# Turning the last three feed-forward tiles with VectorE and small DMAs instead of TensorE, in a fused cross-attention and feed-forward kernel

## The chip, the cores and the metric

The kernel runs on one core of a Trainium2 chip. The metric is device time in microseconds (us): the median of several runs, lower is better. The engines of the core are TensorE (PE), VectorE (DVE), ScalarE (ACT), GpSimd (POOL) and SyncE (SP, which only issues DMAs here).

## What is computed

One transformer block over 1024 tokens (16 sequences of 64) of width 512, in float32: cross-attention with 32 heads of width 128, and a feed-forward layer with a routed low-rank part. The reference, cut to what matters:

```python
x = x + xattn(layernorm(x), ctx, mask, bias, Wq, Wk, Wv, Wo)
x = x + ffn(layernorm(x), ...)

def ffn(x, base_W, base_b, router_W, router_b, A, B, expert_map):
    base_out = einsum('btd,od->bto', x, base_W) + base_b
    logits = einsum('btd,nd->btn', x, router_W) + router_b      # 15 logits
    probs = softmax(logits)
    topk_p, topk_i = top_k(probs, 8)
    w = einsum('btk,btke->bte', topk_p, onehot(expert_map[topk_i]))
    h = einsum('btd,erd->bter', x, A)                           # 8 experts, rank 16
    lora = einsum('bter,eor->bto', h * w[..., None], B) * 2.0
    return base_out + lora
```

## The kernel before

Nearly all of the time goes to the attention projections. The change touches only the last stage, the feed-forward layer.

Tokens are split into eight tiles of 128 (`NT = 8`). For a matmul the normalised tile `xn` (128 tokens by 512) must stand with its width along the partitions, so it is turned: four TensorE transposes of 128x128 into one PSUM bank (`transposed`, line 104, called by `ffn_in`). `split` (lines 70 and 71) then makes two float32r tiles of it: `x2h`, a rounded copy written by ACT, and `x2l`, the rest, written by DVE. Every product is three matmuls (high x high, high x low, low x high).

One tile t goes through these steps:

- `ffn_norm(t)` (lines 700 to 720) and `ffn_apply(t)` (lines 721 to 726): layer norm of the attention's result `acc`. For tiles 5 to 7 the sums are made on ACT and the reciprocal root on POOL (lines 717 and 718).
- `turned(t)`: `ffn_bias` on POOL (line 729, `xb = acc + bias`), then `ffn_in`, the transposes and the split.
- `first(t)`: 12 matmuls of 256 columns (A), the low-rank and router products and the first 112 output columns (line 742).
- `ffn_route` on DVE and ACT (lines 753 to 757): logits, their maximum, exponentials. `ffn_weight` on DVE (lines 762 to 773): the eight best, the experts' weights, and `hw`, the weighted low-rank activations.
- 12 matmuls of 400 columns (B, the rest of the output), `ffn_turn` between them (line 779: one TensorE transpose of `hw`, split into `hh` on ACT and `hl` on DVE), and six matmuls with `hh` and `hl` (`ffn_lora`).
- `ffn_out` (lines 794 to 798): two DVE adds into `o1`, and a DMA to `out` issued by SP.

The stage is software-pipelined by hand. Inside `tc.manual_schedule` each engine runs its instructions in the order in which the program lists them. Round t of the last loop turns tile t+2, does `first` for tile t+1 and finishes tile t:

```python
for t in range(NT):
    turned(t + 2)
    first(t + 1)
    ...
    hh, hl = ffn_turn(hw)
    ffn_mm(po, *x2s[t], B, range(n, KC))
    if 5 <= t + 4 < NT:
        ffn_apply(t + 4)
    if 5 <= t + 5 < NT:
        ffn_norm(t + 5)
```

So in one round ACT runs, in this order: x2h of tile t+2, the exponentials of tile t+1, hh of tile t, then the norms of later tiles. DVE runs x2l, the logits, hl, the routing weights, and the two output adds. Pools give `x2h`, `x2l` and `xb` three buffers and `xn` four.

The same turn by DVE and DMAs is used in the attention stage for `xT` (`x_turn`, lines 330 and 333): one DVE transpose of 32x32 blocks, then 16 DMAs, all issued by POOL, move the blocks to their partitions. SP issues DMAs of a similar kind for the attention's probabilities (`turned_p`, line 505).

Of the kernel before, what the change touches and what calls it, by code (L numbers as in the profile page):

```python
# [9 lines left out]
F32 = mybir.dt.float32  # L10
# [9 lines left out]
P = 128  # L20
D = 512
KC = D // P
H = 32
NT = 8
# [23 lines left out]
def xattn_ffn_kernel(ctx: ExitStack, tc: tile.TileContext, x, ctxT, wq, wk, wv, wo, fside, mask,  # L48
                     base_wT, base_b, arT, router_b, lora_b, expert_map, out):
    nc = tc.nc  # L50
# [12 lines left out]
    def bank(k=None):  # L63
        return psp.tile([P, 512], F32, tag="ps", name="ps")
# [4 lines left out]
    def split(hi, lo, src, lo_eng=None):  # L69
        first = nc.scalar.copy(hi, src)  # L70
        return first, (lo_eng or nc.vector).tensor_tensor(lo, src, hi.bitcast(F32), ALU.subtract)  # L71
# [30 lines left out]
    def transposed(ps, xn):  # L102
        for kc in range(KC):
            nc.tensor.transpose(ps[:, kc * P:(kc + 1) * P], xn[:, kc * P:(kc + 1) * P], ident)  # L104
# [4 lines left out]
    with ExitStack() as actx:  # L109
# [240 lines left out]
        with tc.manual_schedule(engines={nc.tensor.engine}):  # L350
# [159 lines left out]
            def pv_mm(i, pt, v, home="o"):  # L510
                ps = [bank() for _ in range(2)]
                for t in range(NT):
                    for a in range(2):
                        r = slice(a * S, (a + 1) * S)
                        for d in range(0, P, S):
                            c = slice(i * P + d, i * P + d + S)
                            nc.tensor.matmul(ps[a][d:d + S, t * S:(t + 1) * S], lhsT=v[t // 2][r, t % 2, c],  # L517
                                             rhs=pt[r, :, t, :], start=True, stop=True)
                res = []
                for b in range(2):  # L520
                    hl = [blk(home, f"o{c}", F32R) for c in "hl"]
                    with tc.high_priority(offset=SOON):
                        evicted[:] = split(hl[0], hl[1], ps[b])
                    res.append(hl)
                return res

            def proj_o(t, cts, w):
                ps = bank()
                b, g = divmod(t, 4)
                c = slice(g * P, (g + 1) * P)  # L530
                for i, ct in enumerate(cts):
                    mm3(ps, [a[:, c] for a in ct[b]], w[i], i == 0, i == 1)
                with tc.high_priority(offset=SOON):
                    return nc.vector.tensor_tensor(acc[:, t, :], acc[:, t, :], ps, ALU.add)  # L534
# [59 lines left out]
            w, prev, added, pts, soft, ss, ns, t = None, None, None, [], [], [], 0, 0  # L594
# [12 lines left out]
            for p in range(NP):  # L607
# [3 lines left out]
                for c in steps:  # L611
                    if c == "P":
                        old, told = prev, t
                        prev, t = ([pv_mm(i, pts[i], v, "g" if p + 1 == NP else "o") for i in range(2)], w), 0
# [66 lines left out]
    fs2 = ctx.enter_context(tc.tile_pool(name="fs2", bufs=2, reuse_waits="tile"))  # L681
    psf = ctx.enter_context(tc.tile_pool(name="psf", bufs=2, space=PSUM, reuse_waits="tile"))
# [17 lines left out]
    def ffn_norm(t):  # L700
        xt = acc[:, t, :]
        xns[t] = xn = fs2.tile([P, D], F32, tag="xn", name="xn2", bufs=4)
        st = fs2.tile([P, 5], F32, tag="st", name="st", bufs=4)
        total, nm, sq, rs, nb = (st[:, i:i + 1] for i in range(5))
        if t < 5:
            with tc.high_priority(offset=SOON):
                bs = fs2.tile([P, 6], F32, tag="bs", name="bs")
                nc.vector.bn_stats(bs, xt)  # L708
                nc.vector.bn_aggr(st[:, 0:2], bs)
                nc.vector.tensor_scalar(rs, nm, EPS, None, ALU.add)  # L710
                nc.gpsimd.tensor_tensor(rs, rs, nhalf[:, 0:1], ALU.pow)  # L711
                nc.vector.scalar_tensor_tensor(nb, total, -1.0, rs, ALU.mult, ALU.mult)
        else:
            nc.scalar.activation(xn, xt, AF.Identity, accum_out=total)
            nc.scalar.activation(nm, total, AF.Identity, scale=-1.0 / D)
            nc.scalar.activation(xn, xt, AF.Square, bias=nm, accum_out=sq)
            nc.gpsimd.tensor_scalar(rs, sq, 1.0 / D, EPS, ALU.mult, ALU.add)
            nc.gpsimd.tensor_tensor(rs, rs, nhalf[:, 0:1], ALU.pow)
        stats[t] = nm, rs, nb

    def ffn_apply(t):
        nm, rs, nb = stats[t]
        if t >= 5:
            nc.scalar.activation(nb, nm, AF.Identity, scale=rs)
        nc.scalar.activation(xns[t], acc[:, t, :], AF.Identity, bias=nb, scale=rs)

    def ffn_bias(t):
        xb = fs2.tile([P, D], F32, tag="xb", name="xb", bufs=3)
        nc.gpsimd.tensor_tensor(xb, acc[:, t, :], bb, ALU.add)
        return xb  # L730

    def ffn_in(xn):
        ps = psf.tile([P, D], F32, tag="pt", name="pt")
        transposed(ps, xn)
        x2h = fs2.tile([P, D], F32R, tag="x2h", name="x2h", bufs=3)
        x2l = fs2.tile([P, D], F32R, tag="x2l", name="x2l", bufs=3)
        with tc.high_priority(offset=SOON):
            split(x2h, x2l, ps)
        return x2h, x2l

    def mm(o, a, b, start=False, stop=False):
        nc.tensor.matmul(o, lhsT=a, rhs=b, start=start, stop=stop, skip_group_check=True)  # L742

    def ffn_mm(o, x2h, x2l, w, kcs=range(KC)):
        for kc in kcs:
            c = slice(kc * P, (kc + 1) * P)
            mm(o, x2h[:, c], bh[:, kc, w], kc == 0)
            mm(o, x2h[:, c], bl[:, kc, w])
            mm(o, x2l[:, c], bh[:, kc, w], stop=kc == KC - 1)

    def ffn_route(pa):
        lg = fs2.tile([P, NR], F32, tag="lg", name="lg")
        nc.vector.tensor_tensor(lg, pa[:, E * R:NAR], rb, ALU.add)
        nm = fs2.tile([P, 1], F32, tag="nm", name="nm")
        nc.vector.tensor_reduce(nm, lg, AX.X, ALU.max, negate=True)
        sme = fs2.tile([P, 1], F32, tag="sme", name="sme2")
        nc.scalar.activation(lg, lg, AF.Exp, bias=nm, accum_out=sme)
        return pa, lg, sme
# [18 lines left out]
    def ffn_turn(hw):  # L777
        pt = psf.tile([P, D], F32, tag="pt", name="pt")
        nc.tensor.transpose(pt[:, 0:P], hw.rearrange("p e r -> p (e r)"), ident)
        hh = fs2.tile([P, P], F32R, tag="hh", name="hh")  # L780
        hl = fs2.tile([P, P], F32R, tag="hl", name="hl")
        with tc.high_priority(offset=SOON):
            split(hh, hl, pt[:, 0:P])
        return hh, hl

    def ffn_lora(o, hh, hl, w):
        mm(o, hh, lbh[:, w])
        mm(o, hh, lbl[:, w])
        mm(o, hl, lbh[:, w], stop=True)

    def ffn_out(t, xb, pa, po):
        o1 = fs2.tile([P, D], F32, tag="o1", name="o1", bufs=4)
        for c, src in ((slice(NA - NB, D), po), (slice(0, NA - NB), pa[:, NB:NA])):
            nc.vector.tensor_tensor(o1[:, c], xb[:, c], src, ALU.add)
            if t + 1 == NT:
                (nc.sync if c.start else nc.scalar).dma_start(out=out[t, :, c], in_=o1[:, c])
        if t + 1 < NT:
            nc.sync.dma_start(out=out[t], in_=o1)

    xns, xbs, x2s, pas, stats = ({} for _ in range(5))  # L800

    def out_norm(t):
        proj_o(t, *prev)
# [2 lines left out]
    def turned(t):  # L806
        if t < NT:
            xbs[t] = ffn_bias(t)
            x2s[t] = ffn_in(xns[t])

    def first(t):
        if t < NT:
            pas[t] = bank()
            ffn_mm(pas[t][:, A], *x2s[t], A)
# [17 lines left out]
    with tc.manual_schedule(engines=fixed | {nc.vector.engine}):  # L832
# [3 lines that stand above are left out]
            if t == 0:  # L836
                proj_o(7, *prev)
            if t + 1 < NT:
                r = ffn_route(pas[t + 1])
            n = 1 if t else 2  # L840
            po = bank()[:, 0:NF - NA]
            ffn_mm(po, *x2s[t], B, range(n))
# [6 lines that stand above are left out]
            if t + 1 < NT:  # L849
                hw = ffn_weight(*r)  # L850
            ffn_lora(po, hh, hl, B)
            ffn_lora(pas[t][:, A], hh, hl, A)
            ffn_out(t, xbs[t], pas[t], po)


# [40 lines left out]
```

## Time and profile before

| | |
|---|---|
| median of 3 runs | 762.75 us (762.65 to 764.97) |
| the profiled execution | 763.53 us |
| its span in the profile | 761.7 us |
| granted TensorE clock | 0.999 |
| DVE busy | 565.8 us, 74% of the span |
| ACT busy | 412.0 us, 54% |
| POOL busy | 194.8 us, 26% |
| the last loop, eight rounds | from 718.5 to 758.9 us |

The span is what the instruction trace covers; the execution is longer by the time around it. In the profile's lines PE is the matmul and PEld the weight load, which overlaps it; a letter q behind an engine (SPq, ACTq) is its sequencer, which issues DMAs and waits for semaphores. `L742` is line 742 of the kernel. In a timeline the columns are the start in us from the span's start, the length in us, the engine, the line, the operation, what it writes and reads, and a count; brackets give the idle time before it and what ended it. Matmuls are pipelined, so a row's length overlaps the next row.

### The profile page before, as it was taken

To read this page: it belongs to the slowest core of one execution; us is meant where nothing else is said; L and a number is where in the kernel's file an instruction comes from. 1 tells how busy PE (TensorE), PEld (TensorE's weight loads), DVE (VectorE), ACT (ScalarE), POOL (GpSimd) and SP (SyncE) were. 2 spreads that over 40 slices of the span, in tenths; PEclk is the share of its full clock that TensorE was granted. 3 is DMA by queue.
4 is the path that set the end of the run, shared out by engine and by line. 5 is a ranking of instruction groups with operands and counts; after the bars stand their busy time and mean duration, and the time that the engine had idled before them with its cause. 6 is when DMAs were issued, how large, how long until landed. Compare 5 with 4: busy or idle time off the path is not lost.

```text
span 761.7 us, 16780 instructions
## 1 busy us (share of the span) xinstructions
PE 752.5 (99%) x6154; PEld 624.9 (82%) x6154; DVE 565.8 (74%) x1076; ACT 412.0 (54%) x1157; POOL 194.8 (26%) x271
## 2 busy tenths in 40 slices
PE   8999999999999999999999999999999999999998
PEld 6888888888788888877888888888888888888898
DVE  7986567666655776869778777787778777878975
ACT  5654444444444445667645565456645765474361
POOL 0000008108820693223220222022211232010330
PEclk9999999999999999999999999999999999999999
DMA  6685647465735446466554465436544564462011
GB/s 255 229 285 186 205 157 229 147 218 179 224 130 187 156 126 225 142 222 217 189 158 149 138 199 167 142 120 201 174 141 134 180 185 140 125 199 84 1 57 56
DMA packets 84946, 126.79 MB, mean 166 GB/s; under 512 B 11776, under 2 KB 35072, under 8 KB 84864
## 3 DMA queue, kind: packets, MB, share of 16 engines
q1 hardware_dynamic: 80624, 123.56, 49.9%
q0 software_dynamic: 4096, 2.11, 1.2%
q8 instruction: 48, 0.79, 0.5%
q14 instruction: 34, 0.28, 0.1%
q10 hardware_dynamic: 144, 0.06, 0.0%
HBM read 83.74 MB, written 35.65 MB: 157 GB/s over the span
## 4 chain that ended last, share of the span: by engine, by line
PE 91%; DVE 3%; POOL 2%; DMA 2%; issue 1%; ACT 0%; SPq 0%; DVEq 0%; ACTq 0%; POOLq 0%
PE ps L259 73%; PE yz L259 5%; PE ps L742 5%; PE ps L517 4%; PE pss L470 4%; POOL xT L333 1%; DMA cT<-in_ctxT 1%; DMA so<-in_wo 0%; DMA xT<-xb 0%; DVE bs L708 0%; DVE gl L71 0%; PE pt L104 0%; DVE s L161 0%; DVE ol L71 0%; POOL st L711 0%
## 5 line engine op out<-in xcount | busy, mean ns | idle before, releaser
L481 ACT ACTIVATE p<-p,nm 128x64 f32<-128x64 f32 x256 | 85.9, 339 | 33.3 <-DVE nm L475 31.0
L534 DVE TENSOR_TENSOR acc<-acc,ps 128x512 f32<-128x512 f32 x128 | 86.8, 681 | 21.2 <-PE ps L259 20.4
L259 PE MATMUL ps<-wh,ol 128*128 128x512 f32 x256 | 99.9, 390 | 0.8 <-DVE ol L71 0.8
L259 PE MATMUL ps<-wh,oh 128*128 128x512 f32 x256 | 100.1, 391 | 0.0
L259 PE MATMUL ps<-wl,oh 128*128 128x512 f32 x256 | 99.7, 389 | 0.0
L70 ACT CAST gh<-s 128x512 fp32r<-128x512 f32 (+1 forms) x128 | 64.4, 514 | 56.0 <-PE ps L259 45.7
L333 POOL DMA_DIRECT2D xT<-xb x128 | 69.7, 552 | 84.9 <-DVE xb L330 80.7
L71 DVE TENSOR_TENSOR gl<-s,gh 128x512 fp32r<-128x512 f32 (+1 forms) x128 | 72.0, 566 | 23.2 <-ACT gh L70 23.1
L161 POOL TENSOR_TENSOR s<-rq 128x256 f32<-128x256 f32 x32 | 25.3, 790 | 238.9 <-DMA rq<-in_wq 190.1
L71 DVE TENSOR_TENSOR ol<-ps,oh 128x512 fp32r<-128x512 f32 x64 | 39.9, 683 | 31.5 <-ACT oh L70 31.3
L70 ACT CAST gh<-raw 128x512 fp32r<-128x512 f32 x48 | 29.8, 623 | 52.8 <-PE yz L259 36.1
L259 PEld LDWEIGHTS ps<-wh,ol 128*128 128x128 f32 x256 | 48.1, 188 | 11.4 <-DVE ol L71 1.6
L259 PEld LDWEIGHTS ps<-wl,oh 128*128 128x128 f32 x256 | 48.1, 188 | 10.0
L259 PEld LDWEIGHTS ps<-wh,oh 128*128 128x128 f32 x256 | 48.0, 188 | 10.0
L71 DVE TENSOR_TENSOR gl<-raw,gh 128x512 fp32r<-128x512 f32 x48 | 35.1, 731 | 27.9 <-ACT gh L70 20.7
L461 POOL TENSOR_TENSOR bm<-bm,maskb 128x512 f32<-128x512 f32 x32 | 42.4, 1348 | 36.6 <-DMA bm<-in_fside 36.6
L481 ACT ACTIVATION_READ_ACCUMULATOR p<-p,nm 128x1 f32 x256 | 48.6, 190 | 0.0
L565 DVE TENSOR_TENSOR q<-u,ps 128x512 f32<-128x512 f32 x48 | 32.8, 683 | 20.4 <-PE ps L259 16.0
L70 ACT CAST oh<-ps 128x512 fp32r<-128x512 f32 x64 | 33.2, 590 | 11.0 <-PE ps L517 11.0
L70 ACT CAST gh<-rq 128x256 fp32r<-128x256 f32 x48 | 19.5, 406 | 36.0 <-PE ps L259 32.1
L517 PEld LDWEIGHTS ps<-pt,v 64*64 64x64 f32 x2048 | 31.9, 135 | 5.7 <-issue 5.6
L554 ACT COPY u<-ps 128x512 f32<-128x512 f32 x48 | 27.9, 581 | 15.9 <-PE ps L259 8.8
(258 smaller groups left out, 1986.2 us busy)
## 6 DMA issues: line engine op xcount, KB each, us to landing
kd<-c SPq DMA_DIRECT2D x64, 256.0 KB, 2.6
vd<-c SPq DMA_DIRECT2D x64, 256.0 KB, 2.8
kT<-kd SPq DMA_DIRECT2D x64, 256.0 KB, 3.9
v<-vd SPq DMA_DIRECT2D x64, 256.0 KB, 3.7
raw<-in_wk SPq DMA_DIRECT2D x32, 256.0 KB, 4.0
raw<-in_wv SPq DMA_DIRECT2D x32, 256.0 KB, 4.3
rq<-in_wq SPq DMA_DIRECT2D x32, 256.0 KB, 4.1
bm<-in_fside SPq DMA_DIRECT2D x32, 256.0 KB, 4.5
```

Source lines behind the costliest of these rows:

```text
L70: first = nc.scalar.copy(hi, src)
L71: return first, (lo_eng or nc.vector).tensor_tensor(lo, src, hi.bitcast(F32), ALU.subtract)
L259: nc.tensor.matmul(o, lhsT=a, rhs=b, start=first and n == 0, stop=last and n == 2, skip_group_check=True)
L333: nc.gpsimd.dma_start(out=dst[32 * j:32 * j + 32, :, 32 * i:32 * i + 32], in_=xb[32 * i:32 * i + 32, j])
L461: nc.gpsimd.tensor_tensor(bm, bm, maskb, ALU.add)
L470: nc.tensor.matmul(ps[a * S:(a + 1) * S, t, :], lhsT=qT[n // 8][:, cq], rhs=kT[m // 8][:, ck], start=True, stop=True)
L481: nc.scalar.activation(p[:, t, :], p[:, t, :], AF.Exp, bias=nm[:, t:t + 1], accum_out=sme[:, t:t + 1])
L517: nc.tensor.matmul(ps[a][d:d + S, t * S:(t + 1) * S], lhsT=v[t // 2][r, t % 2, c], rhs=pt[r, :, t, :], start=True, stop=True)
L534: return nc.vector.tensor_tensor(acc[:, t, :], acc[:, t, :], ps, ALU.add)
L554: copy = nc.scalar.copy(s[i], b["x"])
L565: add = nc.vector.tensor_tensor(self.blocks[key], s[u], b[bk], ALU.add)
L742: nc.tensor.matmul(o, lhsT=a, rhs=b, start=start, stop=stop, skip_group_check=True)
```

## The change

The new function `ffn_spread(t)` turns a tile without TensorE. DVE transposes 32x32 blocks of `xn` into `x3`. Then 16 DMAs, each of 32 partitions by 512 bytes, move the blocks to the partitions where they belong, into `x4`. Of each four, two are issued by POOL and two by SP. It is called at the end of rounds 1, 2 and 3, for tiles 5, 6 and 7, just ahead of `ffn_out`. `ffn_in` then takes `x4` from SBUF in place of the transposes' PSUM bank when a tile has one. `x3` and `x4` have two buffers each. The rest of the program is as it was; lines below the change move down by 15 to 17.

```diff
+    def ffn_spread(t):
+
+        x3 = fs2.tile([P, 4, KC, 32], F32, tag="x3", name="x3")
+        nc.vector.transpose(x3, xns[t].rearrange("p (k j i) -> p j k i", k=KC, j=4))
+        x4s[t] = fs2.tile([P, 4, KC, 32], F32, tag="x4", name="x4")
+        for j in range(4):
+            for i in range(4):
+                (nc.sync if i % 2 else nc.gpsimd).dma_start(out=x4s[t][32 * j:32 * j + 32, i],
+                                                            in_=x3[32 * i:32 * i + 32, j])
+
-    def ffn_in(xn):
-        ps = psf.tile([P, D], F32, tag="pt", name="pt")
-        transposed(ps, xn)
+    def ffn_in(xn, x4=None):
+        if x4 is None:
+            ps = psf.tile([P, D], F32, tag="pt", name="pt")
+            transposed(ps, xn)
         x2h = fs2.tile([P, D], F32R, tag="x2h", name="x2h", bufs=3)
         x2l = fs2.tile([P, D], F32R, tag="x2l", name="x2l", bufs=3)
         with tc.high_priority(offset=SOON):
-            split(x2h, x2l, ps)
+            if x4 is None:
+                split(x2h, x2l, ps)
+            else:
+                split(*(a.rearrange("p (k i c) -> p k i c", k=KC, i=4) for a in (x2h, x2l)),
+                      x4.rearrange("p i k c -> p k i c"))
         return x2h, x2l
...
     def turned(t):
         if t < NT:
             xbs[t] = ffn_bias(t)
-            x2s[t] = ffn_in(xns[t])
+            x2s[t] = ffn_in(xns[t], x4s.get(t))
...
             ffn_lora(pas[t][:, A], hh, hl, A)
+            if 5 <= t + 4 < NT:
+                ffn_spread(t + 4)
             ffn_out(t, xbs[t], pas[t], po)
```

More of the change, by code (lines that the diff above doesn't have):

```diff
@@ L798, in ffn_out @@
             nc.sync.dma_start(out=out[t], in_=o1)
-    xns, xbs, x2s, pas, stats = ({} for _ in range(5))
+    xns, xbs, x2s, x4s, pas, stats = ({} for _ in range(6))
     def out_norm(t):
```

## The prediction

> **What bounds the kernel now.** I read the busy table first, then the chain of work that ended last, then stretches of one loop round, then the queues of ScalarE (ACT), GpSimd (POOL) and SyncE (SP). The busy table and the chain's first line:
>
> ```profile
> PE 752.5 (99%) x6154; PEld 624.9 (82%) x6154; DVE 565.8 (74%) x1076; ACT 412.0 (54%) x1157; POOL 194.8 (26%) x271
> ...
> PE 91%; DVE 3%; POOL 2%; DMA 2%; issue 1%; ACT 0%; SPq 0%; DVEq 0%; ACTq 0%; POOLq 0%
> ```
>
> TensorE (PE) has no idle time to give; time is won only by taking work off it. The chain in order of time, near the end, with start, length and what:
>
> ```profile
> 735.51 0.44 PE pt L104 x4
> 735.95 1.96 PE ps L742 x15
> 737.90 0.11 PE pt L779
> 738.01 2.54 PE ps L742 x15
> 740.55 0.44 PE pt L104 x4
> ...
> 748.10 4.50 PE ps L742 x30
> ```
>
> A round of the last loop is four transposes (L104), 15 matmuls, one small transpose (L779), 15 matmuls. Stretches of one round each (length, PE, weight load, DVE, ACT, POOL, clock, DMA share, GB/s):
>
> ```profile
> 735.35:740.39 5.04, 5.04 (x38) 4.99 (x37) 3.53 (x15) 2.79 (x8) 2.00 (x3) 1.00 0.13 52
> 740.39:745.43 5.04, 5.04 (x38) 4.99 (x37) 3.52 (x15) 1.14 (x4) 1.30 (x1) 1.00 0.15 55
> 745.43:750.47 5.04, 5.04 (x38) 4.99 (x36) 3.51 (x15) 1.14 (x4) 1.29 (x1) 1.00 0.13 52
> 750.47:755.07 4.60, 4.60 (x33) 4.55 (x32) 2.76 (x14) 0.55 (x3) 0.00 (x0) 1.00 0.15 57
> ```
>
> These are rounds 3 to 6 (t = 3..6). Round 6 turns no tile and shows what a round costs without the transposes: 4.60 against 5.04.
>
> **What is removed.** Tiles 5, 6 and 7 are turned in rounds 3, 4 and 5 (`turned(t + 2)`). The change takes 12 PE transposes out, 0.44 us a round by both views: 3 x 0.44 = **1.32 us** at the very most, 0.17% of the time. PE gains nothing else.
>
> **What is added, and the cheap parts.** Per tile one DVE transpose. It is not in this stage, but its twin for xT (L330, same shape and same view) takes 0.70 us. It stands behind the routing weights and ahead of the two output adds. In the rounds that follow DVE waits 0.59 us for ACT before x2l, so 0.1 us is left over; the next use of that is a hw wanted over 2 us later: nothing on the path. If DVE had no such gap it would be 0.7 us per round at most. x2h and x2l read SBUF in place of PSUM: rows of that kind take 0.62 and 0.73 us where the old took 0.59 and 0.69, taken as nothing beside what follows.
>
> **The costly part: when the turned tile is there.** Tile t+4 is spread at the end of round t and wanted as ACT's first item of round t+2. Between them lie 16 DMAs, 8 through SP and 8 through POOL. Rows for both kinds, the nearest there are (32 partitions, SBUF to SBUF; ns min/median/max):
>
> ```profile
> L505 SPq DMA_DIRECT2D pt<-pb x128: 507/582/1426, 335.6 to 699.7; - x128
> ...
> DMA to landing us min/median/max: 1.7/1.9/3.8
> ```
>
> ```profile
> L333 POOL DMA_DIRECT2D xT<-xb x128: 548/548/742, 114.9 to 271.2; - x128
> ...
> DMA to landing us min/median/max: 1.6/2.6/5.0
> ```
>
> On SP, four in a row near 693.0 start 0.57, 0.63 and 0.63 us apart and land 1.88 us after the issue (median). On POOL, 15 in a row take 8.12 us, 0.54 each, and land after 1.67 us when other traffic is small, as it is here (0.13 to 0.15 of the DMA engines).
>
> A rule of the Trainium skill bears on this ("DMA: Bandwidth & Descriptors", section "Issuing engines are not separate DMA queues"): starting DMAs from several engines only saves the sequencer's issue time, "usually small relative to the DMA itself"; its section on the anatomy of a DMA gives about 2.0 us plus bytes over 436 GB/s. By the rule 16 KB land 2.04 us after tile 5's transpose, at 733, three microseconds early, and the sum is -1.32. By the rows, issue is not small: 8 x 0.63 = 5.0 us on SP and 8 x 0.54 = 4.3 us on POOL for each tile, longer than the transfer. I take the rows.
>
> What is queued behind the wait? ACT is in order: x2h (now waiting for 16 DMAs), then the exponentials of the routing, then hh, which PE needs for its last six matmuls *in the same round*. DVE's x2l and routing sums stand in the same line. The old rows of round 3 (ACT):
>
> ```profile
> 735.98 0.59 ACT L70 CAST x2h<-pt 128x512 fp32r<-128x512 f32 x1
> 737.81 0.31 ACT L757 ACTIVATE lg<-lg,nm 128x15 f32<-128x15 f32 x1 [1.23 <-DVE nm L755]
> 738.02 0.19 ACT L757 ACTIVATION_READ_ACCUMULATOR lg<-lg,nm 128x1 f32 x1
> 738.11 0.24 ACT L70 CAST hh<-pt 128x128 fp32r<-128x128 f32 x1
> ```
>
> From x2h's start L: x2l +0.63 (735.98 to 736.61), lg +0.61 (726.75 to 727.36, where nothing else holds it), exponential +0.42, hh +0.30, its length 0.25 and 0.04 to PE: hh is there at L + 2.25. In a short round PE wants it 3.71 after the start (754.18 - 750.47). So **x2h may start 1.46 us into the round for nothing**; later, PE stands still and the round ends at L + 2.25 + 0.11 (first matmul after a wait, as at 724.26) + 0.89 (rest, 755.07 - 754.18) = L + 3.25. The idle 1.23 us of ACT above is the old cover.
>
> Two more terms. ACT clears the 16 semaphores two at a time; in front of the copy at 697.27 the clears started about 0.077 us apart. In the built order the last POOL DMA of each tile is in the first pair, so seven pairs follow it, 0.54 + 0.04. And POOL's own work lies between its batches:
>
> ```profile
> 731.13 0.19 POOL L717 TENSOR_SCALAR st<-st 128x1 f32<-128x1 f32 x1 [2.92 <-ACT xn L716]
> 731.41 0.55 POOL L718 TENSOR_TENSOR st<-st,nhalf 128x1 f32<-128x1 f32 x1
> 731.92 1.29 POOL L729 TENSOR_TENSOR xb<-acc,bb 128x512 f32<-128x512 f32 x1
> ```
>
> POOL needs 4.3 + 1.3 + 0.8 = 6.4 us for a round that lasts 4.6 to 5.0: it falls further behind with each tile. SP needs 5.0 + 0.5 for its `out` DMA, also too much.
>
> **The sum**
> - Tile 5: DVE transpose 730.22 to 730.92. SP starts 730.96, its last 735.31, landed 737.19. POOL starts behind L718 at 731.96, its last 735.74, landed 737.41. L = 737.41 + 0.58 = 738.0; the limit was 735.35 + 1.46 = 736.81. Round 3 ends 741.25, not 739.95.
> - Tile 6: POOL free 736.28, xb to 737.57, L717 and L718 to 738.4, last DMA 742.18, landed 743.85, L = 744.43 against a limit of 742.71. Round 4 ends 747.68.
> - Tile 7: its DVE transpose waits behind round 3's late routing: hl 2.28 after L, hw and transpose to 4.9 after, 742.9. POOL ends tile 6 at 742.72, xb at 744.0, last DMA 747.79, landed 749.46, L = 750.04 (SP: landed 749.17, about 749.7). Round 5 ends 750.04 + 3.25 = 753.29, where it ended at 750.47: **+2.82 us**. Rounds 6 and 7 follow unchanged; xb of tiles 6 and 7 comes by 751, wanted after 757.
>
> The profiled execution took 763.53 (span 761.70 and 1.83 around it): 766.35 by the sum. It lies 0.78 above the median 762.75; the difference goes on the median: about **765.5**.
>
> **Ends of the unknown prices.** POOL's new DMAs write 32 pieces of 512 B, where the row wrote 128 of 128 B: perhaps cheaper, down to the 0.33 us of an `out` issue on SP, perhaps not. I take 0.54, the only POOL row. SP's 0.63 moved 1 KB pieces of the same 32 partitions; its lower end is the 0.47 of v loads. Landing: 1.67, up to the 2.6 median of busy windows, and one row near 699 took 3.3 while an instruction fetch ran.
>
> **Rivals**
> - *SP sets the pace* (POOL at 0.33): tile 5 lands by SP at 737.19, L 737.25; tile 6 landed 742.6, L 743.2; tile 7's transpose ready 742.15, landed 748.4, L 748.9; end 752.15: +1.7, **764.4**. For it: fewer pieces. Against: 548 ns is minimum and median alike, like a fixed cost. Within 0.3% of before.
> - *The DMAs land in time* (the other side). Place: x2h of tile 5 must start by 736.81; price: issue under about 0.47 on both queues. Then tile 5 is there at 736.2, rounds 3 and 4 are short, only tile 7 is some 0.7 late or not at all: -0.5 to -1.32, **761.4 to 762.2**. For it: ACT idles 1.23 us there, DMA engines idle. Against: 128 SP rows have a minimum of 507 ns.
> - *Slower landing*: 0.9 us more on each landing and an instruction fetch of about 1 us (one of 0.99 ran at 742.7) on one of the last: +3.7 to +5, **766.5 to 767.8**. For it: 48 more DMAs to fetch; against: quiet traffic.
>
> **How the numbers follow.** POOL sets the pace 0.48 (765.5, its own range 764.9 to 766.4), SP sets it 0.25, slower landing 0.15, in time 0.12. About 0.3% (2.3 us) is what a measurement tells from no change. Faster by more is out of reach of a 1.32 us gain: 0.02 for the measurement alone. Slower by more, above 765.04: most of the first case and all of the third, 0.60; within: 0.38. Range: leaving out the in-time case and the far end of slow landing, 763.3 to 767.8.
>
> **What would show it.** PE: rounds 3 to 5 without L104, each with one gap ahead of the first lora matmul, released by ACT hh, 1.2, 1.7 and 0.9 us (after the round's start is shifted). ACT: x2h of tiles 5, 6, 7 released by a DMA at about 738.0, 744.4, 750.0. POOL: 24 DMAs, rows near 0.54; SP: 24 near 0.6. Wrong would be: no gap ahead of the lora matmuls (the DMAs were in time), POOL rows near 0.3 with SP landing last, or gaps in front of the A matmuls of the next round, which I expect to have x2h early enough.

## The result, and the profile after

The changed kernel took 767.65 us (median of 7 runs, 765.36 to 769.68) against 763.01 us for the kernel before (7 runs, 762.64 to 764.97). The ratio of the runs is 1.0047 with a 95% interval of 1.0032 to 1.0062: about 3.6 us slower. The two medians are 4.64 us apart, over seven runs that scatter by up to 4.3 us; the text goes by the ratio, which has an interval. The profiled execution took 768.67 us with a span of 766.9 us, 5.2 us more than the span before.

Not all of those 5.2 us belong to the change. PE stopped for 1.86 us near 497.6, in the attention stage, which the change doesn't touch; such stops come and go from run to run. The last stage begins 1.30 us later than before, which is no part of the change's cost. So two profiles are compared here by one **stretch**, from the start of the transpose of `hw` in round 1 (L779, after the change L794) to the start of the last row of output adds on DVE (L794, after the change L809). It is 30.51 us before and 34.24 us after, **+3.73 us**, which agrees with the ratio of the timed runs. Where a time of after is set beside one of the prediction, on the scale of before, 1.30 us are taken off it.

The busy table of after and the first line of its chain of waits:

```profile
PE 752.5 (98%) x6142; PEld 623.3 (81%) x6142; DVE 563.9 (74%) x1079; ACT 411.7 (54%) x1157; POOL 206.2 (27%) x295
...
PE 87%; DVE 5%; POOL 3%; issue 2%; DMA 1%; ACT 1%; SPq 1%; ACTq 0%; DVEq 0%; POOLq 0%
```

PE has its 12 transposes less (6154 to 6142 matmuls) and its share of the chain has fallen from 91% to 87%; DVE, POOL, ACT, issue and SP's queue have what it lost. Where PE stands still is in its timeline (start, length, engine, line, what, and in brackets the idle time before and what ended it):

```profile
741.35 0.45 PE L757 MATMUL ps<-lbh,hh 128*128 128x400 f32 x1 [0.83 <-ACT hh L70]
...
747.70 0.45 PE L757 MATMUL ps<-lbh,hh 128*128 128x400 f32 x1 [1.48 <-ACT hh L70]
...
754.50 0.45 PE L757 MATMUL ps<-lbh,hh 128*128 128x400 f32 x1 [1.95 <-ACT hh L70]
```

There are three stops, one in each of rounds 3, 4 and 5, each ahead of the first matmul with `hh`. The stage before has none. Why `hh` is late is in ACT's timeline:

```profile
739.08 0.62 ACT L70 CAST x2h<-x 128x512 fp32r<-128x512 f32 x1 [1.73 <-PE pt L794]
740.74 0.31 ACT L772 ACTIVATE lg<-lg,nm 128x15 f32<-128x15 f32 x1 [1.04 <-DVE nm L770]
...
741.05 0.24 ACT L70 CAST hh<-pt 128x128 fp32r<-128x128 f32 x1
...
745.43 0.62 ACT L70 CAST x2h<-x 128x512 fp32r<-128x512 f32 x1 [3.09 <-DMA out<-o]
...
752.24 0.62 ACT L70 CAST x2h<-x 128x512 fp32r<-128x512 f32 x1 [4.60 <-DMA out<-o]
```

`x2h` waits, and `hh` stands 1.97 us behind it in the same queue. The releaser in the brackets is not to be trusted here: `x2h` waits for 16 DMAs at once, and it starts 0.44 to 0.60 us after the last of them has landed (738.64, 744.83 and 751.68). The `hw` transpose and the `out` DMA merely came near that moment.

The queues that issue those DMAs, POOL first and then SP. A row with x8 is one tile's batch, with the time from the first issue to the end of the last:

```profile
733.30 4.02 POOL L739 DMA_DIRECT2D x<-x  x8
737.34 1.30 POOL L729 TENSOR_TENSOR xb<-acc,bb 128x512 f32<-128x512 f32 x1
738.74 0.18 POOL L717 TENSOR_SCALAR st<-st 128x1 f32<-128x1 f32 x1
739.00 0.56 POOL L718 TENSOR_TENSOR st<-st,nhalf 128x1 f32<-128x1 f32 x1
739.53 4.02 POOL L739 DMA_DIRECT2D x<-x  x8
```

```profile
732.21 5.07 SPq L739 DMA_DIRECT2D x<-x  x8
737.37 0.53 SPq L813 DMA_DIRECT2D out<-o  x1
738.00 4.94 SPq L739 DMA_DIRECT2D x<-x  x8
```

Both queues work almost without a break for the whole of the three rounds; tile 6's batch starts when tile 5's and what stands behind it are done. The one gap is on SP, 0.35 us ahead of tile 7's batch (743.92): there SP waits for the tile's DVE transpose, which ended at 743.87, late behind round 3's late routing. All 48 DMAs together (duration min/median/max in ns, then the landing):

```profile
L739 SPq DMA_DIRECT2D x<-x x24: 507/588/705, 732.2 to 748.3; - x24
L739 POOL DMA_DIRECT2D x<-x x24: 496/496/585, 733.3 to 748.2; - x24
...
DMA to landing us min/median/max: 1.6/1.8/3.7
```

The maximum of 3.7 is no stray: the last four DMAs of tile 7, issued from 747.65 to 748.28, all landed between 751.17 and 751.68, after 3.3 to 3.7 us. The queues from 745 to 755 show one guest (in the first line each number is what the DMA engines moved in a quarter of a microsecond):

```profile
GB/s 64 2 12 107 12 78 54 68 64 62 51 80 4 105 27 103 86 62 62 0 6 10 0 57 385 385 393 385 385 107 0 0 0 0 0 0 0 0 0 0
...
q8 instruction: 1, 0.02, 0.6%
```

It is one packet of 16,384 bytes, an instruction fetch, from 749.10, 1.03 us long. The DMA engines are not short of bandwidth beside it: from 749.75 to 750.75 they move 0 to 10 GB/s. The records of single packets show more. Fifteen sixteenths of each of the four late DMAs had gone by 749.77. Then no packet starts until 750.13, where the fetch's packet ends, and from there to 750.51 the last sixteenths follow, ten packets one by one. So each of the four seems to have had one part in 16 in line behind the fetch.

What each round cost is the distance between `hw` transposes. A round without its transposes takes 4.60 us (round 6 before), so the loss per round is what lies above that:

| lost over 4.60 us | predicted | after | the change again |
|---|---|---|---|
| round 3 (tile 5 late) | 1.30 | 1.12 | 1.11 |
| round 4 (tile 6 late) | 1.83 | 1.72 | 2.29 |
| round 5 (tile 7 late) | 1.01 | 2.22 | 1.74 |
| less three rounds' transposes | -1.32 | -1.32 | -1.32 |
| sum | 2.82 | 3.74 | 3.82 |

"The change again" is a second profile of the same kernel, one of the runs below. In the first profile each loss is the stop shown above and 0.24 to 0.29 us with which PE starts up again: the first matmul after a stop takes 0.28 us to the next one where 0.18 is usual, and the rest was not followed up.

### The profile page after: what moved, and what is told of

The parts are those of the page before. It is cut to its first block, busy times and chain, and to the rows that moved or that the text cites. A ratio compares the mean times of both kernels' runs of the same rounds, so it can differ in the third digit from the quotient of the medians.

```text
span 766.9 us, 16869 instructions
## 1 busy us (share of the span) xinstructions
PE 752.5 (98%) x6142; PEld 623.3 (81%) x6142; DVE 563.9 (74%) x1079; ACT 411.7 (54%) x1157; POOL 206.2 (27%) x295
## 4 chain that ended last, share of the span: by engine, by line
PE 87%; DVE 5%; POOL 3%; issue 2%; DMA 1%; ACT 1%; SPq 1%; ACTq 0%; DVEq 0%; POOLq 0%
PE ps L259 72%; PE yz L259 5%; PE ps L517 4%; PE pss L470 4%; POOL xT L333 2%; PE ps L757 1%; DMA x<-x 1%; DMA cT<-in_ctxT 1%; SPq L739 0%; POOL x L739 0%; DVE acc L534 0%; DVE bs L708 0%; DVE gl L71 0%; POOL st L711 0%; DVE x2l L71 0%
## 5 line engine op out<-in xcount | busy, mean ns | idle before, releaser
L70 ACT CAST gh<-rq 128x256 fp32r<-128x256 f32 x48 | 19.5, 405 | 36.2 <-PE ps L259 32.2
L470 PEld LDWEIGHTS pss<-kT,q 128*64 128x64 f32 x1024 | 31.3, 138 | 6.5 <-issue 5.3
```

The costliest lines, as they stand in the source:

```text
L470: nc.tensor.matmul(ps[a * S:(a + 1) * S, t, :], lhsT=qT[n // 8][:, cq], rhs=kT[m // 8][:, ck], start=True, stop=True)
```

## The experiments

Each kernel is the change with the edit shown. Its stretch is set beside 30.51 us (before) and 34.24 (after); in the timed ones the ratio to before says the same with an interval.

### A second profile of the change

The change, unaltered.

> The changed kernel once more, for its profile: in the first one the last four DMAs of tile 7 took 3.3 to 3.7 us to land, beside an instruction fetch of 1.03 us, where the others took 1.6 to 2.1. If that is chance: the stretch is about 33.3 us (before plus 2.8, the predicted sum). If it belongs to the change: again 34.2.

This one run took 767.46 us, with a stretch of 34.34. The landing is slow again: an instruction fetch starts at 748.35, and a DMA issued at 747.01 lands after 3.36 us. So the late landing is part of the change, not an accident of one execution. Tile 6 was 0.55 us later here, because its last POOL DMA landed after 2.33 us and not 1.78; it was issued 0.15 us behind the 256 KB `out` DMA. POOL's `xb` ran beside DVE here: L782, a small DVE instruction of the routing weights, took 1.12 us in place of 0.17, and tile 7's `x2l` 0.82 in place of 0.69, so that the last `hh` stood 2.10 us behind its `x2h` and not 1.97.

### The DMAs without anyone who waits for them

```diff
-            x2s[t] = ffn_in(xns[t], x4s.get(t))
+            x2s[t] = ffn_in(xns[t])
```

> The three VectorE transposes and the 48 DMAs stay, but nobody reads x4: x2h and x2l come from TensorE transposes, as before. Theory (late arrival: the small DMAs take too long to issue, and ScalarE's x2h, then hh, then TensorE wait for them): no wait is left, so the time is that of before, between -0.3 and +0.7 us (763.0 to 763.7); the profile shows no gap ahead of the lora matmuls. Rival 1 (the DMAs themselves, their traffic, instruction fetches, or GpSimd's late xb, slow the stage): it stays at +2 us or more. Rival 2 (the cost is in x2h and x2l reading SBUF behind 16 semaphores): also the time of before, so this run doesn't tell it from the theory.

764.07 us against 764.39, ratio 0.9993 (0.9977 to 1.0010), stretch 30.51: to the hundredth the kernel before. The DVE transposes, the 48 DMAs, their traffic and the late `xb` on POOL cost nothing here. The loss needs somebody who reads `x4`: it is in the wait for the data, or in reading them from SBUF, and the next run bears on the second.

### Neither turn

```diff
-            if 5 <= t + 4 < NT:
-                ffn_spread(t + 4)
...
-            x2s[t] = ffn_in(xns[t], x4s.get(t))
+            x2s[t] = ffn_in(xns[t], xns[t] if t > 4 else None)
...
-                split(*(a.rearrange("p (k i c) -> p k i c", k=KC, i=4) for a in (x2h, x2l)),
-                      x4.rearrange("p i k c -> p k i c"))
+                split(x2h, x2l, x4)
```

> Leaves out the turn of tiles 5, 6 and 7 altogether: no transposes, no DMAs, x2h and x2l are split from the unturned xn in SBUF, so the output of these tiles is another function. Theory: the upper bound of the gain, 3 x 0.44 = 1.32 us less than before, about 761.7; rounds 3 to 5 take 4.60 us each. Rival 2 (reading SBUF in place of PSUM costs on ScalarE and VectorE): no faster than before, rounds near 5.0.

763.31 us, ratio 0.9982 (0.9969 to 0.9994), stretch 29.25. This is the most that the removal of 12 transposes can bring, 1.26 us; the prediction had put it at 1.32. `x2h` and `x2l` read SBUF here (the latter in 0.68 to 0.69 us, as from PSUM), so reading SBUF alone is no part of the change's loss.

### All 16 DMAs on SP

```diff
-                (nc.sync if i % 2 else nc.gpsimd).dma_start(out=x4s[t][32 * j:32 * j + 32, i],
+                nc.sync.dma_start(out=x4s[t][32 * j:32 * j + 32, i],
```

> All 16 DMAs of a tile are issued by SyncE: doubles the suspected issue cost on one queue and takes it off GpSimd. Theory (issue at 0.63 us each sets the arrival): 48 x 0.63 plus two out DMAs between them, the last lands near 763.4 on the scale of before, round 5 ends near 766.9 instead of 750.5: +16 us, about 779. Rivals (landing, traffic or semaphores and not issue): the same 48 transfers, so within 1 us of the change, about 767.

783.19 us, ratio 1.0252 (1.0216 to 1.0288), stretch 49.99, +19.5. `x2h` started at 742.40, 753.16 and 764.66: the issue rate of the rows carries through to the start of the data's use, within about a microsecond over three tiles. The loss was 3 us larger than expected. That microsecond is a part of it, and the windows show the larger part (length, PE, weight load, DVE, ACT, POOL, granted clock, DMA share, GB/s):

```profile
746.00:748.00 2.00, 2.00 (x12) 2.00 (x11) 1.80 (x5) 0.00 (x0) 0.09 (x1) 0.50 0.10 25
...
767.00:769.00 2.00, 2.00 (x8) 1.99 (x9) 1.82 (x10) 0.00 (x0) 0.00 (x0) 0.50 0.00 0
```

After stops of 5.17, 4.36 and 5.33 us the granted clock is 0.50. The stops of up to 1.95 us in the change leave it at 1.00, as in this window behind its third stop:

```profile
754.00:760.00 6.00, 5.50 (x37) 5.42 (x38) 4.43 (x22) 1.00 (x6) 0.00 (x0) 1.00 0.11 44
```

The Trainium skill ("TensorE: Matmul & The Clock Gate", Part 1) puts the point at one idle window of about 3.4 us, which fits both; no stop in this stage lay between 2.01 and 4.36 us.

### The split moved behind `hh`

If `hh` is late only because it queues behind `x2h`, `x2h` can go behind it:

```diff
         if t < NT:
             xbs[t] = ffn_bias(t)
-            x2s[t] = ffn_in(xns[t], x4s.get(t))
+            if t < 5:
+                x2s[t] = ffn_in(xns[t])
...
             hh, hl = ffn_turn(hw)
+            if 5 <= t + 2 < NT:
+                x2s[t + 2] = ffn_in(xns[t + 2], x4s[t + 2])
```

> As the change, but for tiles 5 to 7 x2h stands behind hh on ScalarE and x2l behind hl on VectorE, so that the DMA wait no longer holds up the same round's hh. The DMAs are not touched. Theory: the deadline of x4 moves from 1.46 us into the round to about its end, 2.5 us later. Tile 5 (ready at 738.0 by the times of before) costs nothing, tile 6 about 0.4, tile 7 about 1.1 us; less the 1.32: about +0.2 us against before (-0.7 to +1.2), 2.5 to 3.5 less than the change. If lateness alone counted and not what is queued behind the wait: as the change, +3.6. Rival 1 (traffic): as the change, too.

765.61 us, ratio 1.0022 (1.0006 to 1.0038), stretch 32.24. Half of the loss is gone, but the expectation was too good by about 1.5 us. No stop is left ahead of `hh`; PE now waits for the tile itself:

```profile
744.82 0.38 PE L757 MATMUL ps<-bh,x2h 128*128 128x256 f32 x1 [0.61 <-ACT x2h L70]
```

So the queue on ACT is about half of the price. That the issue rate alone is too slow does not follow from what is left. This stop is tile 6's, whose last DMA landed after 2.36 us; it was issued 0.13 us behind the `out` DMA, as in the second profile. And tile 7 met a fetch here too, from 745.87, 1.46 us long: seven of its DMAs landed after 2.8 to 4.0 us.

### Only tile 7

```diff
-            if 5 <= t + 4 < NT:
+            if t + 4 == 7:
                 ffn_spread(t + 4)
```

> Only tile 7 is spread, with its 16 DMAs as in the change; tiles 5 and 6 are turned by TensorE. Theory (the queues fall behind from tile to tile): without the two tiles ahead of it tile 7 starts at 741.0 on both queues, lands by 746.2 on GpSimd and 747.2 on SyncE, x2h at 747.3 to 747.8 against a limit of 746.9: 0.4 to 0.9 us late, less the 0.44: 0 to +0.6 us, the stretch 30.4 to 31.1. If every spread tile costs the same, backlog or not: a third of the change, +1.2 us, 31.7.

765.94 us, ratio 1.0023 (1.0006 to 1.0039), stretch 32.02. Meant to show the backlog, it decides nothing about it: the fetch came at 742.96, lasted 1.24 us and fell in the middle of this tile's DMAs. They landed after up to 3.8 us, and one issue on SP took 1.62 us. The round of this single tile lost 1.95 us, not much less than tile 7's 2.22 behind two others in the change, and that pointed to the fetch.

### The fetch

In the trace a 16,384-byte instruction packet appears once in this part of the stage in every run. The page of the change counts 48 of them, for 12,284 matmuls and weight loads on PE: one for each 256. Early in the program each comes, give or take ten, at the same count of PE matmuls started by then, whatever the run. So the packets are taken to be PE's, each near its own place in PE's instructions.

The packet of the last stage stands at 6053 before, at 6053 with the DMAs unread, and at 6065 in both profiles of the change. At an unchanged count it would have come 8 matmuls later in the *work*, because 8 of the 12 transposes stood ahead of it. It came 20 later. The other 12 the removal doesn't explain: with the turn left out, the same 12 transposes fewer, the count is 6057. What moved it further is not shown. The later place in the work, and the stops in rounds 3 and 4, bring it from 742.72, where nobody waited for a DMA, to 749.10, where tile 7's last DMAs are under way.

If PE's place sets it, 16 matmuls fewer at the very start of the program should push it 16 further on in the work, past tile 7:

```diff
-WARM = 18
+WARM = 2
```

> The change with 16 fewer warm-up matmuls at the start of the program (2 in place of 18), so that every later place in PE's instruction stream comes 16 matmuls earlier in the stream's count and a 16,384-byte fetch that follows PE's position falls 16 matmuls later in the work. Theory (the last tile's late landing is that fetch): the fetch of the last stage leaves 749.1 and comes about 2.5 us later (16 matmuls of 0.15 to 0.18 us), after tile 7's DMAs have landed; these then land in 1.6 to 2.1 us, x2h of tile 7 starts near 749.5 to 750.1 on the scale of the kernel before, and the stretch from round 1's hw transpose to the last output add is 33.0 to 33.4 us (34.24 and 34.34 in the change's two profiles, 30.51 before). Rival (the DMAs of tile 7 are late for another reason, such as the queue's backlog): the landings stay at 3.3 to 3.7 us and the stretch at 34.2. A third outcome: the fetch doesn't move, and nothing is told apart. The total may differ by what the start does with fewer warm-up matmuls, so the stretch is read, not the total.

The fetch moved, to 758.33. Its count is 6066, as in the change, with 16 matmuls fewer ahead of it. Tile 7's last DMA had landed at 756.14, 2.2 us earlier. (Three earlier packets show the same: 463, 586 and 713 in the change, 461, 587 and 716 here.) The landings of all 48 DMAs, a DVE row, the copy of tile 7 and PE's third stop:

```profile
DMA to landing us min/median/max: 1.6/1.7/2.3
...
755.05 1.13 DVE L782 TENSOR_TENSOR lg<-lg,rest 128x15 f32<-128x15 f32 x1
...
756.70 0.62 ACT L70 CAST x2h<-x 128x512 fp32r<-128x512 f32 x1 [2.43 <-DMA x<-x]
...
759.40 0.45 PE L757 MATMUL ps<-lbh,hh 128*128 128x400 f32 x1 [0.17 <-ACT hh L70]
```

The maximum is 2.3 where it was 3.7, the third stop 0.17 where it was 1.95, and the stretch 33.09, inside the expectation. `x2h` of tile 7 starts at 749.34 on the scale of before, a little ahead of what was expected. The losses of rounds 3 to 5 are now 1.15, 2.30 and 0.46, with the transposes a sum of 2.59. **With the fetch off tile 7's landing, 1.15 us of the change's 3.73 are gone** (1.25 beside the second profile, whose tile 6 was as late as here: 2.29 and 2.30). It is one run against each. The `out` DMA is no rival: SP issues it 0.70 us behind tile 7's last DMA in both, at 748.98 in the change and at 755.06 here.

What is left of the third stop is not the DMAs' either. L782 took 1.13 us in place of 0.17 beside POOL's `xb` (754.84 to 756.14), so DVE came to `x2l` 1.08 us after the start of `x2h` and not 0.65.

The whole run was slower (773.53 us): PE stopped for 2.89 us after the shorter warm-up, and for 1.75 and 2.03 us in the attention stage. As a version of the kernel it is no good; the stretch is what it was made for.

### Fewer DMAs, through DRAM

If the count of DMAs is the cost, 5 in place of 16 should end it: one writes `x3` to DRAM, four read it back turned (two by SP, two by POOL).

```diff
+        xd = dram.tile([4, 32, 4, KC * 32], F32, tag=f"xd{t}", name=f"xd{t}")
+        nc.sync.dma_start(out=xd.rearrange("i r j e -> (i r) j e"), in_=x3.rearrange("p j k c -> p j (k c)"))
         for j in range(4):
-            for i in range(4):
-                (nc.sync if i % 2 else nc.gpsimd).dma_start(out=x4s[t][32 * j:32 * j + 32, i],
-                                                            in_=x3[32 * i:32 * i + 32, j])
+            (nc.sync if j % 2 else nc.gpsimd).dma_start(
+                out=x4s[t][32 * j:32 * j + 32].rearrange("p i k c -> p i (k c)"),
+                in_=xd[:, :, j].rearrange("i r e -> r i e"))
```

> The order of the change, but the blocks move through DRAM: one 256 KB write of x3 by SyncE and four reads of 32 partitions, two by SyncE, two by GpSimd: 5 DMAs per tile in place of 16. Theory (issue time and the queues' backlog): write landed 2.1 us after the transpose, two reads 0.6 apart, landed 2.0 to 2.6 later: x4 is there 4.9 us after the transpose, on the scale of before 735.9, 740.9 and 745.9 against limits of 736.8, 741.4 and 746.0. No stall or a few tenths on tile 7: -1.3 to -0.6 us against before; the stretch from round 1's hw transpose to the last output add, 30.51 us before and 34.24 in the change, is 29.25 to 29.9. If a DMA chain as such, whatever its number of issues, costs: +2 us or more.

766.92 us, ratio 1.0047 (1.0026 to 1.0067), stretch 32.33: no better than the change by the timed runs, and a miss by 2.4 us or more. Two DMAs in a row, a write and a read, take too long for a copy that must start early in the round; the DVE instruction of L782 (L784 in this kernel) took 1.09 us beside POOL's `xb`, at 741.01; and a fetch at 747.39 made tile 7's reads land after 2.8 to 3.1 us in place of 1.8 to 2.3. So the same with the split behind `hh`, as above:

> Through DRAM as in the run before it, and x2h behind hh, x2l behind hl. Theory: x4 is early by 2 us or more everywhere, no gap at all; -1.3 us against before, the stretch is 29.25 us, as with the unturned tiles. This is the version that could beat both kernels, by no more than 0.17%, less than a timing tells. If something in reading x4 or in the five DMAs costs: 30 us or more.

767.19 us, ratio 1.0034 (1.0020 to 1.0049), stretch 33.34: missed again, by another mechanism. `x2h` is in time, but `hw` is not:

```profile
742.41 1.91 DVE L786 TENSOR_TENSOR we<-oneh,lg 128x120 f32<-128x120 f32 x1
742.87 1.29 POOL L729 TENSOR_TENSOR xb<-acc,bb 128x512 f32<-128x512 f32 x1
```

A DVE instruction that usually takes 0.28 us took 1.91 beside POOL's `xb`, which POOL's waits for the DRAM write had pushed to this place; PE stopped for 1.28 us ahead of the `hw` transpose, and for 1.31 in the next round. The Trainium skill has a rule for that ("SBUF — State Buffer", section "Who interferes with whom"): a DVE instruction with two SBUF inputs and a GpSimd instruction that reads SBUF shut each other out. If the rule holds, POOL must be left alone. All five DMAs go to SP (an edit of the run just shown):

```diff
-            (nc.sync if j % 2 else nc.gpsimd).dma_start(
+            nc.sync.dma_start(
```

> As the run through DRAM with the split behind hh, but all five DMAs of a tile are issued by SyncE, so that GpSimd's order and times are those of before. In the run before it, VectorE's two-input add of the routing took 1.91 us in place of 0.28 while GpSimd's late xb ran (742.87 to 744.16), and TensorE waited 1.28 us for hw. Theory (with GpSimd left alone xb runs early in the round, and nothing collides): no such row, hw in time, no gap; the stretch from round 1's hw transpose to the last output add is 29.3 us (before 30.51), -1.2 us against before. If the VectorE rows were slow for another reason (the DMAs, x2l's place): 31 us or more, gaps ahead of hw stay.

763.19 us against 763.90, ratio **0.9980 (0.9966 to 0.9995)**, stretch 30.02. This version is ahead of both kernels, of the one before by little: 0.49 us in the stretch of one profile, and 0.4 to 2.6 us by the interval of the timed runs. The same DVE instruction in it:

```profile
747.89 0.28 DVE L786 TENSOR_TENSOR we<-oneh,lg 128x120 f32<-128x120 f32 x1
```

`xb` had run before it (from 745.18, 1.28 us long), and PE has no stop ahead of an `hw` transpose. What is left to lose is the fetch once more: at 747.57, 1.45 us long, it lay on tile 7's reads (landed after 3.4 to 3.5 us, one issue on SP 1.93 us long). The same with 2 warm-up matmuls:

> The version that turns tiles 5 to 7 through DRAM with all five DMAs of a tile on SP and makes x2h and x2l behind hh of the round before, again with 2 warm-up matmuls in place of 18. It lost 0.77 us of the stretch where the fetch at 747.57 made tile 7's reads land in 3.4 us. Theory: the fetch comes about 2.5 us later, tile 7's reads land in about 2 us, and the stretch falls from 30.02 to 29.2 to 29.5 (29.25 with the turn left out). Rival: the reads still land late and the stretch stays at 30.0. The total may differ by what the start does, so the stretch is read.

The fetch came at 751.36, all reads landed after 1.9 to 2.0 us, PE had no stop in these rounds, and the stretch was 29.25, exactly that with the turn left out. In its one run the total was 764.87 (763.19 for one run of the kernel before beside it), with the cost of the shorter warm-up in it; a way to move the fetch without that cost was not tried.

Last, five DMAs on SP with the split where the change has it:

> As the run before it, with x2h and x2l in the place that they have in the change, first in the round. Theory: 1 write and 4 reads on SyncE land 5.2 to 5.75 us after the tile's VectorE transpose, on the scale of before 736.2 to 736.7, 741.2 to 741.7 and 746.2 to 746.7, against limits of 736.8, 741.4 and 746.0: a stall of 0 to 0.3, 0 to 0.3 and 0.2 to 0.7 us; the stretch is 29.4 to 30.6 us. It tells what the place in ScalarE's order is worth when the transfer is just about in time: the difference to the run before it.

765.60 us, ratio 1.0016 (0.9998 to 1.0034), stretch 32.03: worse than expected. Tile 5 was in time for `x2h`, but the split's second half reads `x4` and `x2h`, both in SBUF, and met `xb` (PE stopped for 0.47 us):

```profile
736.61 1.28 POOL L729 TENSOR_TENSOR xb<-acc,bb 128x512 f32<-128x512 f32 x1
...
736.93 1.51 DVE L71 TENSOR_TENSOR x2l<-x,x2h 128x512 fp32r<-128x512 f32 x1 [0.71 <-ACT x2h L70]
```

Alone it takes 0.69. Tile 7 was again late by a fetch (at 745.80, reads landed after 2.9 to 3.4 us, a stop of 1.75 us).

## Why the prediction was right, and where its size was off

The predicted time was 765.5 us and the measured 767.65; the range held it, its upper end by 0.15 us, and slower by more than 0.3% was the likeliest outcome named. The likeliest case's own range ended at 766.4, below what came. That the range held is in part luck: its upper end was meant for landings that are all 0.9 us slower, which didn't come, and of the 4.64 us between the medians the stretch accounts for 3.73.

- **The gain.** 1.32 us predicted as the most, 1.26 measured with the turn left out.
- **The cheap parts at nothing.** Right in the first profile of the change: the run with the DMAs unread has before's stretch. That `x2l` reads SBUF was taken as nothing too; that held only where `xb` didn't run beside it. In the second profile it did, for 0.28 us, and `hh` came 0.13 us later; in the last run above it cost more.
- **Issue is not small.** The rows were taken and not the rule that issue time is "usually small relative to the DMA itself". SP's 0.63 us from one issue to the next was met, POOL's 0.54 came out as 0.49. The run with all 16 on SP confirms the rate; by the rule it would have been a gain. The landing itself (median 1.8) was no longer than the 2.04 us that the prediction had estimated from the rule's page.
- **The chain** from `x2h` over the exponentials to `hh`: 2.00 us predicted from copy to copy, 1.97 measured. `x2h` was expected at 738.0, 744.4 and 750.0, and started at 737.78, 744.13 and 750.94. Tile 7's DVE transpose, expected to end at 742.9 behind round 3's late routing, ended at 742.57, and SP waited for it. The clearing of the semaphores, 0.58 us, was 0.44 to 0.60. No stop in front of the next round's A matmuls: right.
- **The term that was mis-sized** is tile 7's "last DMA 747.79, landed 749.46", and in it the landing of 1.67 us. By POOL's cheaper issue the last DMAs were issued earlier than thought, at 746.93 and 746.98 on the scale of before, but they landed after 3.3 to 3.4 us. With the fetch out of the way tile 7's last four DMAs land after 1.6 to 1.9 us and the sum is 2.59 against the 2.82 predicted. So the mechanism and the issue terms were right, and the fetch is what put the sum of 3.74 above the forecast. The 0.2 us that are then left the other way are not one term: POOL's issue was cheaper, while tile 6's last DMA landed after 2.3 us (1.67 taken) in two of three profiles, and `xb` met DVE.
- **The rivals.** "Slower landing" had the fetch in it, at a chance of 0.15, and its range of 766.5 to 767.8 holds the result. Its other half, 0.9 us more on each landing, did not happen (median 1.8). "SP sets the pace" was half true: with POOL at 0.49 the two queues' last landings lie within 0.5 us of each other, SP's last for tiles 5 and 7, POOL's for tile 6. "In time" fell.

The fetch was in the profile before, at 742.72, and the prediction treated where it would fall as chance. It was not all chance: its place follows PE's instructions, of which the change takes some out, and the stops that the sum itself forecast moved it further, into tile 7's DMAs. But the removal accounts for only 8 of the 20 matmuls by which it came later.

That the packets are PE's is inferred from their number and their places in the streams. The places are not exact: with 16 warm-up matmuls fewer the packet came 17 matmuls later in the work in the change, and 29 later in the version through DRAM (counts 6061 and 6074); and in the attention stage several packets kept their place in the work and not their count (5822 in the change, 5807 with 16 matmuls fewer). That a part of each late DMA stood behind the fetch's packet is read from the times of the packets; on which DMA engine a packet ran is not in this trace. POOL went from one batch to the next in 6.23 us where 6.4 were predicted, so it does fall behind; what that costs apart from the first tile's own lateness was not separated, as the run for it met a fetch.

## What to carry to other kernels

A turn by 16 small DMAs costs 16 issues, here 0.49 us each on POOL and 0.63 on SP, and what counts is the time from the first issue to the last landing against the slack of the *first* instruction in the queue that waits for it; put such a wait behind whatever the bottleneck engine needs in the same round. Before moving work onto POOL or into SBUF operands on DVE, look at which two-input DVE instructions will run beside which POOL instructions. When instructions are removed from a stream, ask also what fetch of that stream moves, and onto what.

## What the runs showed that was not expected

- An instruction fetch of 16,384 bytes takes 0.9 to 1.5 us on the DMA engines' queue. In the runs where it fell on small DMAs, some of these landed 1 to 2 us later, with their last packets starting only when the fetch's packet ended, and an issue on SP beside it took up to 1.99 us (the split moved behind `hh`) in place of 0.6.
- Beside POOL's `xb` (1.3 us), DVE instructions with two SBUF inputs took 1.91 us (usually 0.28), 1.51 (usually 0.69) and 1.13 (usually 0.17). It goes the other way too: where `x2l` had started 0.15 us before it (742.46 and 742.61, five DMAs on SP with the split in its old place), `xb` took 1.67 us.
- After stops of 4.4 to 5.3 us the granted clock was 0.50 for 3 us and more; after stops of up to 2.0 us it stayed at 1.00.
- With sixteen DMAs to wait for, ACT starts 0.44 to 0.60 us after the last has landed.
